# Graph layer with one-hot matmuls: all matmuls of a block in 128x32 tiles, and the normalisation in steps of its own

## The chip, the cores and the metric

The kernel runs on one core of a Trainium2 chip. The metric is the time of one execution on the device in microseconds; the kernel before takes 783.06 us (median of 3 runs, 783.03 to 785.78).

## What is computed

There are 6,250 nodes with 128 features and 100,000 edges, sorted by destination, of two types. Each edge sends its source's row, multiplied by one of two weight matrices, to its destination:

```python
Xs = X[src]
m_data = Xs @ W_data.T + b_data
m_ctrl = Xs @ W_control.T + b_control
msg = jnp.where((edge_types == 0)[:, None], m_data, m_ctrl)
agg = jax.ops.segment_sum(msg, dst, num_segments=X.shape[0])
out = jax.nn.relu(agg + (X @ W_self.T + b_self))
x = _layernorm(x + out, axis=-1)
```

## The kernel before

**Precision.** Every f32 value that goes through a matmul is kept as three bf16 parts whose sum is the value: `w3` (weights), `x3` (the transposed input), `m3` (the messages). A product of x and W is nine matmuls, one for each pair of parts.

**Prologue** (to about 118 us). The tables of messages are built for all nodes and both types: `multiply()` makes y = x W + b for a block of 128 nodes (L411, L414), `split_a` to `split_d` cut it into three parts in `m3`, which stays in SBUF: 98 tiles of 128 messages by 384 (three parts of 128). It also goes to a DRAM table. Constants are built at the start on VectorE while a transfer of the edges' rows (`er`) is under way.

**Groups.** Destinations are taken in 49 blocks of 128 nodes, in ten groups of 4, 5, 5, ... blocks. Before a group's blocks are summed its edges are put into slots: an edge of block q whose source lies in tile s of the 98 gets one of R = 32 slots of (q, s). A window of 18 x 128 edges per block is loaded. For each k of KT = 18, `bucket_hots` (L514, VectorE) makes `hot_st`, a one-hot of the source tile for 128 edges and all the blocks of the group, with the block index q innermost: reading one block's columns is a stride of n elements. `ranks` (L528 and L533, through the helper `by_columns` at L202, and L531) counts the slots. `fill_a` makes `two`, the one-hot of the slot times the source row and times the destination row. `fill_b` (L567) multiplies the two: for each k and q, `hot_st` is the stationary operand (128 columns), `two` is streamed (64 columns: 32 slots by two values). The result in PSUM holds, for every source tile, its slots' values.

`fill_c` copies it to `vs` (L580), writes the source rows to DRAM as `packed` (L582) in the order tile, slot, and turns the destination rows with small matmuls (L590) into `to`. Edges that found no slot are listed (to L661) and their messages fetched from the DRAM table into `msg_s` (32 rows), with `hot_s` as their one-hot of destinations.

**A block.** `spread` reads the block's row of `packed` back, broadcast to 128 partitions (`rows`, L697). `select` (L706, VectorE, two halves) turns it into one-hots of the source row. `to_hots` (L718) makes the one-hots of destinations, `hot_d`. Then for each of 25 buckets g of four source tiles: `gather` (L734) fetches the messages of 4 x 32 slots, each matmul with 32 columns of weights in its own column tile of TensorE; `evict` (L743, ScalarE) copies them as bf16 to `gs`; `add_up` (L753, through L202) adds them to the destinations in `agg` with `by_columns`, which cuts the 128 columns of weights into four matmuls of 32. The last bucket has 64 rows only. After it, one matmul of 32 rows by 128 columns adds the spilled edges (L757). `own_of` adds x W_self and its bias to the first 128 columns of `agg` (L774, L778). `finish_blocks` (VectorE) adds the three parts (L139), applies the relu and adds x (L135); after the last block of a group `norm_and_store` does the statistics, the root (ScalarE, L157), the scaling (L167) and the store (L172).

**Order.** [...] That order is made ahead of time by the planner `Order`: each `step` names the engines that can do it with their costs, what it needs, and (`due`) when it ought to be done. Steps emit their instructions when the planner picks them. The pools matter too: `agg` and `h_p` have one buffer, `g_ps` five, `gs` eight, `rows` four.

Of the kernel before, what the change touches and what calls it, by code (L numbers as in the profile page):

```python
# [38 lines left out]
NS = (NT + 3) // 4  # L39
PARTS = (4, 8, 8, 8, 8, 8, 5)  # L40
KC = 3
DC = 5
SC = 49
# [54 lines left out]
def kernel(  # L98
# [48 lines left out]
    def norm_and_store(h, b0, n, work):  # L147
        mv = work.tile([P, Q, 2], F32, name="mv")
        for j in range(n):
            st = work.tile([P, 6], F32, name="st")  # L150
            nc.vector.bn_stats(st, h[:, j, :])  # L151
            nc.vector.bn_aggr(mv[:, j, :], st)

        v = work.tile([P, Q], F32, name="v")
        nc.vector.tensor_scalar_add(v[:, :n], mv[:, :n, 1], EPS)
        s0 = work.tile([P, Q], F32, name="s0")
        nc.scalar.activation(s0[:, :n], v[:, :n], AF.Sqrt)  # L157
        r0 = work.tile([P, Q], F32, name="r0")
        nc.vector.reciprocal(r0[:, :n], s0[:, :n])
        q = work.tile([P, Q], F32, name="q")  # L160
        nc.vector.tensor_mul(q[:, :n], v[:, :n], r0[:, :n])
        nc.vector.tensor_add(q[:, :n], q[:, :n], s0[:, :n])
        rstd = work.tile([P, Q], F32, name="rstd")
        nc.vector.reciprocal(rstd[:, :n], q[:, :n])
        nc.vector.tensor_scalar_mul(rstd[:, :n], rstd[:, :n], 2.0)
        for j in range(n):
            nc.vector.tensor_scalar(h[:, j, :], h[:, j, :], mv[:, j, 0:1], rstd[:, j : j + 1],  # L167
                                    op0=ALU.subtract, op1=ALU.mult)
        n0 = b0 * P
        full = min(n, (N - n0) // P)  # L170
        if full:
            nc.sync.dma_start(  # L172
                out[n0 : n0 + full * P, :].rearrange("(b p) f -> p b f", p=P), h[:, :full, :]
            )
        if full < n:
            n1 = n0 + full * P
            nc.sync.dma_start(out[n1:N, :], h[: N - n1, full, :])

    with ExitStack() as main:
        sums_over_windows(main, tc, x, xt, edges, w, bias, table, x3_t, packed, total,  # L180
                          finish_parts, load_rows, norm_and_store)

    matched = nc.values_load(total[0:1, 0:1])
    with tc.If(matched != E), ExitStack() as rest:
        sums_over_all(rest, tc, xt, edges, w, bias, table, dram, finish, load_rows, norm_and_store)


def sums_over_windows(ctx, tc, x, xt, edges, w, bias, table, x3_t, packed, total,
                      finish_parts, load_rows, norm_and_store):
# [5 lines left out]
    ctx.enter_context(tc.manual_schedule())  # L195
    order = Order()
# [73 lines left out]
    V.tensor_scalar(rest, tri_f, -1.0, 1.0, op0=ALU.mult, op1=ALU.add)  # L270

    sel = const.tile([P, 4, NS], BF16, name="sel")
    for t in range(4):
        V.tensor_scalar(sel[:, t, :], iota_f[:, t + 1 : t + 1 + 4 * NS : 4], pid, None, op0=ALU.is_equal)
# [15 lines left out]
    three_parts([parts[:, i, :] for i in range(3)], b3, left[:3])  # L290
    bias3 = const.tile([3, D3], BF16, name="bias3")
# [50 lines left out]
    def due(kind, *i):  # L342
        if kind in ("counted", "turned", "first"):
            return 5.0
# [15 lines left out]
        if kind in ("rows", "sel", "d", "g", "e", "s"):  # L360
            of = {"rows": 1, "sel": 2, "d": 5}.get(kind, NS)
            lead = {"rows": -9, "sel": -3, "d": -1, "g": 0, "e": 1, "s": 2}[kind]
            return BUILT + BLOCK * (i[0] + (i[1] / of if len(i) > 1 else 0)) + lead
        n = GROUPS[i[0]]
        end = BUILT + BLOCK * STARTS[i[0]] - AHEAD
        if kind == "norm":
            return end + AHEAD + BLOCK * n + 20
# [187 lines left out]
    def fill_b():  # L555
        for grp, n in enumerate(GROUPS):
            free = [("listed", grp - 1)] if grp else ["first"]
            for c in range(KT // KC):
                yield step(("v", grp, c), {"T": 0.2 + 0.047 * KC * n}, ("two", grp, c), *free)
                if c == 0:  # L560
                    vts[grp] = ps_a.tile([P, 512], F32, name="small")
                vt = vts[grp][:, : n * 2 * R].rearrange("p (q r) -> p q r", q=n)
                two = two_s.pop((grp, c))
                for k in range(c * KC, c * KC + KC):
                    hot = hots.pop((grp, k))
                    for q in range(n):
                        T.matmul(vt[:, q, :], hot[:, :, q],  # L567
                                 two[:, k - c * KC, :, :, q].rearrange("p i r -> p (i r)"),
                                 start=k == 0 and q == 0, stop=k == KT - 1, skip_group_check=True)
                free = []  # L570

    def fill_c():
        for grp, n in enumerate(GROUPS):
# [3 lines left out]
            yield step(("vs", grp), {"A": 0.45}, ("v", grp, KT // KC - 1))  # L577
            vs = work.tile([P, Q, 2 * R], BF16, name="vs")
            vt = vts.pop(grp)
            A.copy(vs[:, :n, :], vt[:, : n * 2 * R].rearrange("p (q r) -> p q r", q=n))  # L580
            yield step(("packed", grp), {"S": 0.2}, ("vs", grp), lag=2.5)
            nc.sync.dma_start(  # L582
                packed[b0 : b0 + n, :].rearrange("q (s r) -> s q r", r=R), vs[1 : NT + 1, :n, :R]
            )
            yield step(("vd", grp), {"T": 0.05 * 4 * n}, ("vs", grp))
            vd = ps_a.tile([P, 512], F32, name="small")
            vd_v = vd[:, : n * NS].rearrange("p (q g) -> p q g", q=n)
            for q in range(n):
                for t in range(4):
                    T.matmul(vd_v[t * R : (t + 1) * R, q, :], vs[:, q, R:], sel[:, t, :],  # L590
                             start=True, stop=True, skip_group_check=True)
# [53 lines left out]
            for c in range(m):  # L645
# [14 lines left out]
            hot_s = work.tile([R, Q * P], BF16, name="hot_s")  # L660
            V.tensor_scalar(hot_s[:, : n * P], iota_f[:R, : n * P], dq, None, op0=ALU.is_equal)  # L661
            yield step(("spilled", grp), {"G": 0.8}, ("listed", grp), *stored, lag=2.5)
            msg_s = work.tile([R, D3], BF16, name="msg_s")
            G.indirect_dma_start(  # L664
                out=msg_s, out_offset=None, in_=table[:, :],
                in_offset=bass.IndirectOffsetOnAxis(ap=row_i[:, 0:1], axis=0),
            )
            spills[grp] = hot_s, msg_s
# [18 lines left out]
    d_hots, g_tiles, gs_tiles, aggs, xss, x3b, hs_ = {}, {}, {}, {}, {}, {}, {}  # L687
# [3 lines left out]
    def spread():  # L691

        for b, (grp, q) in enumerate(blocks):
            free = [("g", b - RB, NS - 1)] if b >= RB else []
            yield step(("rows", b), {"S": 0.1}, ("packed", grp), "built", *free, lag=4.0)
            rows[b] = late.tile([P, NT, R], BF16, name="rows", bufs=RB)
            nc.sync.dma_start(rows[b].rearrange("p s r -> p (s r)"),  # L697
                              packed[b : b + 1, :].to_broadcast([P, NT * R]))

    def select():  # L700

        for b in range(NB):
            for s0 in range(0, NT, SC):
                yield step(("sel", b, s0 // SC), {"V": 0.62}, ("rows", b))
                s = rows[b][:, s0 : min(s0 + SC, NT), :]
                V.tensor_scalar(s, s, pid1, None, op0=ALU.is_equal)  # L706
# [20 lines left out]
    def gather():  # L727
        for i, (b, g) in enumerate(tiles):
            free = [("e", *tiles[i - GB])] if i >= GB else ["built"]
            n = slots_of(g)  # L730
            yield step(("g", b, g), {"T": 0.17}, ("sel", b, (4 * g + n // R - 1) // SC), *free)
            g_tiles[b, g] = g_ps = ps_g.tile([P, 512], F32, name="g_ps")
            for t in range(n // R):
                T.matmul(g_ps[t * R : (t + 1) * R, :D3], rows[b][:, 4 * g + t, :],  # L734
# [10 lines left out]
    def add_up():  # L745
        for b, g in tiles:
            grp, q = blocks[b]
            free = [("agg", b)] if g == 0 else [("spilled", grp), ("o", b)] if g == NS - 1 else []
            yield step(("s", b, g), {"T": 0.17}, ("e", b, g), ("d", b, g // DC), *free)
# [5 lines left out]
            if g == NS - 1:  # L755
                hot_s, msg_s = spills[grp]
                T.matmul(aggs[b], hot_s[:, q * P : (q + 1) * P], msg_s, start=False, stop=True,  # L757
                         skip_group_check=True)
# [9 lines left out]
    def own_of(blocks, begun):  # L768

        for i, b in enumerate(blocks):  # L770
            yield step(("agg", b), {"S": 0.0}, *([("sum", blocks[i - 1])] if i else []))
            yield step(("o", b), {"T": 0.8}, ("xs", b), begun(b))
            own = aggs[b][:, :D]
            T.matmul(own, ones_b[:3, :], bias3[:, 2 * D :], start=False, stop=False,  # L774
                     skip_group_check=True)
            for i in range(3):
                for k in range(3):
                    T.matmul(own, x3b[b][:, i, :], w3[:, k, 2 * D :], start=False, stop=False,  # L778
                             skip_group_check=True)

    def finish_blocks():
        for b, (grp, q) in enumerate(blocks):
            yield step(("sum", b), {"V": 0.85}, ("s", b, NS - 1))
            if q == 0:
                hs_[grp] = late.tile([P, Q, D], F32, name="h_p")
            finish_parts(hs_[grp][:, q, :], aggs.pop(b), xss.pop(b), work)
            if q == GROUPS[grp] - 1:
                yield step(("norm", grp), {"V": 0.5 * GROUPS[grp] + 0.9}, ("sum", b))
                norm_and_store(hs_.pop(grp), STARTS[grp], GROUPS[grp], work)
# [4 lines left out]
    def close_build():  # L794
# [8 lines left out]
        spread(), select(), finish_blocks(), add_up(), gather(), evict(), to_hots(), bucket_hots(),  # L803
# [12 lines left out]
def sums_over_all(ctx, tc, xt, edges, w, bias, table, dram, finish, load_rows, norm_and_store):  # L816
# [3 lines left out]
    ps = ctx.enter_context(tc.tile_pool(name="ps_all", bufs=1, space=PSUM))  # L820
    w_self = const.tile([D, D], F32, name="w_self")
# [63 lines left out]
    for b0 in range(0, NB, Q):  # L885
        n = min(Q, NB - b0)
        h = work.tile([P, Q, D], F32, name="h")
        for j in range(n):
# [9 lines left out]
        norm_and_store(h, b0, n, work)  # L898
# [31 lines left out]
```

## Time and profile before

| | busy us | share of the span |
|---|---|---|
| TensorE matmuls | 718.1 | 92% |
| VectorE | 658.4 | 84% |
| ScalarE | 543.1 | 69% |
| GpSimd | 55.1 | 7% |

The costliest groups of instructions, with busy time, mean of one, and the idle time ahead of them with what ended it:

```profile
L743 ACT CAST gs<-g_ps 128x384 bf16<-128x384 f32 x1225 | 492.3, 498 | 136.2 <-PE g_ps L734 117.7
L734 PE MATMUL g_ps<-m,rows 128*32 128x384 bf16 x4802 | 381.8, 328 | 3.7 <-DVE rows L706 3.3
L718 DVE TENSOR_TENSOR hot_d<-count,to 128x640 bf16<-128x640 bf16 x245 | 132.6, 552 | 16.0 <-PE agg L202 12.3
L706 DVE TENSOR_SCALAR rows<-rows,pid 128x1568 bf16<-128x1568 bf16 x98 | 60.7, 621 | 0.7 <-DMA rows<-packed 0.7
L567 PE MATMUL small<-two,hot_st 128*128 128x64 bf16 x882 | 76.3, 255 | 4.4 <-DVE two L552 4.4
L778 PE MATMUL agg<-w,x_p 128*128 128x128 bf16 x441 | 33.1, 220 | 0.0
```

In a shape such as 128*32 128x384 the first pair is rows by columns of the weights, the second the streamed operand. Matmuls overlap, so the busy time of a group is the time in which at least one runs, and count times mean is much more. PE means TensorE, PEld its weight loads, DVE VectorE, ACT ScalarE, POOL GpSimd, SP the queue from which most transfers start.

### The profile page before, as it was taken

How to read it: one execution, taken by the hardware profiler on the slowest of the kernel's cores; microseconds unless marked ns; L12 is line 12 of the kernel's file. 1: busy time of each engine (PE TensorE's matmuls, PEld its weight loads, DVE VectorE, ACT ScalarE, POOL GpSimd, SP SyncE). 2: the span in 40 equal slices, each digit the busy share in tenths (PEclk: the TensorE clock that was granted, in tenths of full speed). 3: DMA queues.
4: the chain of work that ended last, by engine and by line, in shares of the span. 5: the costliest groups of instructions: out<-in, count | busy, mean ns of one | idle time of the engine just before them, and what ended most of it. 6: DMA issues, size and time to landing. Idle time of an engine off the chain costs nothing.

```text
span 783.7 us, 31989 instructions
## 1 busy us (share of the span) xinstructions
PE 718.1 (92%) x13451; PEld 474.0 (60%) x13451; DVE 658.4 (84%) x1764; ACT 543.1 (69%) x1321; POOL 55.1 (7%) x48
## 2 busy tenths in 40 slices
PE   0989949999999999999999999999998998999993
PEld 0556635665666666566656666666665665666662
DVE  6688878998989998998989899899998999968622
ACT  1445425687787679678777858767786786787993
POOL 2454420000000000000000000000000000000000
PEclk9999978999999999999999999999999999999997
DMA  5455463133105213310431520142052023205200
GB/s 198 121 169 184 165 215 124 25 122 105 44 15 178 74 27 137 112 24 16 176 75 27 181 71 21 32 161 78 16 181 74 11 69 124 82 12 181 69 3 20
DMA packets 60616, 72.93 MB, mean 93 GB/s; under 512 B 15348, under 2 KB 53249, under 8 KB 60417
## 3 DMA queue, kind: packets, MB, share of 16 engines
q1 hardware_dynamic: 58860, 66.69, 25.9%
q10 hardware_dynamic: 1158, 3.41, 1.2%
q8 instruction: 107, 1.75, 0.9%
q0 software_dynamic: 448, 0.72, 0.3%
q14 instruction: 43, 0.35, 0.1%
HBM read 52.85 MB, written 17.96 MB: 90 GB/s over the span
## 4 chain that ended last, share of the span: by engine, by line
PE 70%; DVE 21%; DMA 4%; issue 2%; ACT 1%; SPq 0%; POOL 0%; DVEq 0%; ACTq 0%
PE agg L202 22%; PE g_ps L734 20%; PE small L567 9%; PE acc L202 7%; PE y L414 6%; DVE slot L531 4%; DVE hot_d L718 3%; PE agg L778 3%; DVE rows L706 2%; DVE two L552 2%; PE agg L757 1%; DMA out<-h_p 1%; DMA er<-in_edges,row_i 1%; DMA rows<-packed 1%; DVE st L151 1%
## 5 line engine op out<-in xcount | busy, mean ns | idle before, releaser
L743 ACT CAST gs<-g_ps 128x384 bf16<-128x384 f32 x1225 | 492.3, 498 | 136.2 <-PE g_ps L734 117.7
L202 PE MATMUL agg<-gs,hot_d 128*32 128x384 bf16 (+1 forms) x4900 | 390.1, 332 | 15.7 <-ACT gs L743 15.3
L734 PE MATMUL g_ps<-m,rows 128*32 128x384 bf16 x4802 | 381.8, 328 | 3.7 <-DVE rows L706 3.3
L202 PEld LDWEIGHTS <-hot_d 128*32 128x32 bf16 (+1 forms) x4900 | 179.0, 114 | 103.5 <-issue 33.5
L734 PEld LDWEIGHTS <-rows 128*32 128x32 bf16 x4802 | 143.8, 98 | 61.8 <-issue 12.1
L718 DVE TENSOR_TENSOR hot_d<-count,to 128x640 bf16<-128x640 bf16 x245 | 132.6, 552 | 16.0 <-PE agg L202 12.3
L531 DVE TENSOR_REDUCE slot<-acc 128x5 f32<-128x490 f32 (+1 forms) x180 | 117.6, 653 | 28.3 <-PE acc L202 28.2
L514 DVE TENSOR_TENSOR hot_st<-count,st_b 128x640 bf16<-128x640 bf16 (+1 forms) x180 | 99.3, 568 | 3.1 <-PE small L567 3.1
L567 PE MATMUL small<-two,hot_st 128*128 128x64 bf16 x882 | 76.3, 255 | 4.4 <-DVE two L552 4.4
L567 PEld LDWEIGHTS <-hot_st 128*128 128x128 bf16 x882 | 65.8, 122 | 21.3 <-issue 20.1
L202 PE MATMUL acc<-hot_st,rest 128*32 128x490 bf16 (+1 forms) x720 | 69.9, 371 | 6.7 <-DVE slot L531 6.7
L202 PE MATMUL acc<-hot_st,tri 128*32 128x490 bf16 (+1 forms) x720 | 69.5, 368 | 0.0
L414 PE MATMUL y<-w,x 128*128 128x256 bf16 x441 | 62.9, 292 | 0.4 <-POOL x L397 0.4
L706 DVE TENSOR_SCALAR rows<-rows,pid 128x1568 bf16<-128x1568 bf16 x98 | 60.7, 621 | 0.7 <-DMA rows<-packed 0.7
L139 DVE TENSOR_REDUCE whole<-agg 128x128 f32<-128x384 f32 x49 | 27.2, 556 | 31.4 <-PE agg L757 30.4
L664 POOL DMA_INDIRECT msg_s<-table,row_i x10 | 9.9, 990 | 599.1 <-PE g_ps L734 533.3
L414 PEld LDWEIGHTS <-x 128*128 128x128 bf16 x441 | 41.3, 103 | 13.8 <-issue 1.3
L202 PEld LDWEIGHTS <-rest 128*32 128x32 bf16 x720 | 25.3, 95 | 26.1 <-issue 16.1
L439 ACT CAST m<-yr 128x512 bf16<-128x512 f32 (+1 forms) x25 | 15.2, 609 | 26.5 <-DVE yr L433 26.2
L778 PE MATMUL agg<-w,x_p 128*128 128x128 bf16 x441 | 33.1, 220 | 0.0
L552 DVE TENSOR_TENSOR two<-hr,lo 128x480 bf16<-128x480 bf16 (+1 forms) x60 | 29.0, 484 | 2.1
L552 DVE TENSOR_TENSOR two<-hr,rel_b 128x480 bf16<-128x480 bf16 (+1 forms) x60 | 30.6, 511 | 0.0
(135 smaller groups left out, 449.0 us busy)
## 6 DMA issues: line engine op xcount, KB each, us to landing
rows<-packed SPq DMA_DIRECT2D x49, 784.0 KB
table<-m SPq DMA_DIRECT2D x10, 768.0 KB
x_p<-x_t SPq DMA_DIRECT2D x49, 96.0 KB
x_t<-x SPq DMA_DIRECT2D x5, 768.0 KB
xs_p<-in_x SPq DMA_DIRECT2D x49, 64.0 KB
xt<-in_xt ACTq DMA_DIRECT2D x5, 512.0 KB
out<-h_p SPq DMA_DIRECT2D x8, 320.0 KB
win<-in_edges SPq DMA_DIRECT2D x49, 27.0 KB
```

The costliest lines, as they stand in the source:

```text
L139: nc.vector.tensor_reduce(whole, agg.rearrange("p (i c) -> p c i", i=3), axis=AX.X, op=ALU.add)
L202: T.matmul(out[c : c + 32], lhsT[:, c : c + 32], rhs, **flags)
L414: T.matmul(y[:, j, :], x3s[g][:, b + j - at_part[g], i, :], w3[:, k, : 2 * D], start=False, stop=i == k == 2)
L514: V.tensor_tensor(hot, counted[n], fields[grp][2][:, k, None, :].to_broadcast([P, P, n]), op=ALU.is_equal)
L531: V.tensor_reduce(slots[grp][:, k, :], by_q, axis=AX.X, op=ALU.max)
L552: V.tensor_tensor(two[:, :, i], hr, f[:, ks, None, :].to_broadcast(wide), op=ALU.mult)
L567: T.matmul(vt[:, q, :], hot[:, :, q], two[:, k - c * KC, :, :, q].rearrange("p i r -> p (i r)"), start=k == 0 and q == 0, stop=k == KT - 1 ...
L706: V.tensor_scalar(s, s, pid1, None, op0=ALU.is_equal)
L718: V.tensor_tensor(hot, counted[DC], places[grp][:, q, None, c * DC : c * DC + DC].to_broadcast([P, P, DC]), op=ALU.is_equal)
L734: T.matmul(g_ps[t * R : (t + 1) * R, :D3], rows[b][:, 4 * g + t, :], m3[:, 4 * g + t, :], start=True, stop=True)
L743: (A.copy if e == "A" else V.tensor_copy)(gs[:n], g_tiles.pop((b, g))[:n, :D3])
L778: T.matmul(own, x3b[b][:, i, :], w3[:, k, 2 * D :], start=False, stop=False, skip_group_check=True)
```

## The change

Within a block and its slots, matmuls with 128 columns of weights alternate with those of 32. The change gives those of the slots, of x W_self and of the spilled edges the shape of 128 rows by 32 columns:

- Slots: the operands are swapped. `two` (32 slots of one value of one block) is stationary, `hot_st` is streamed (100 source tiles). Two blocks share a PSUM range, in four column tiles. The result is turned round: slots on partitions, source tiles along the row. So `vs`, `packed` and `rows` are in the order slot, tile, and the weights of `gather` are read from `rows` with a stride of 98 elements. `select` is one instruction a block.
- x W_self: the three parts of the weights are streamed together (384 columns), into all three thirds of `agg`, which are added up later anyway.
- Spilled edges: `hot_s` and `msg_s` are padded to 128 rows; the rows past the 32 are zero but for one that holds the bias of W_self, which replaces L774.
- Normalisation: the statistics are taken after each block. Root, scale, apply and store are planner steps of their own, and the scaling of the rows goes from VectorE to ScalarE as an activation with scale and shift.

```diff
-                yield step(("v", grp, c), {"T": 0.2 + 0.047 * KC * n}, ("two", grp, c), *free)
+                yield step(("v", grp, c), {"T": 0.05 * KC * n}, ("two", grp, c), *free)
...
-                    hot = hots.pop((grp, k))
+                    hot = hots.pop((grp, k))[:, 1 : NC + 1, :]
                     for q in range(n):
-                        T.matmul(vt[:, q, :], hot[:, :, q],
-                                 two[:, k - c * KC, :, :, q].rearrange("p i r -> p (i r)"),
-                                 start=k == 0 and q == 0, stop=k == KT - 1, skip_group_check=True)
+                        for i in range(2):
+                            c0 = (q % 2 * 2 + i) * R
+                            T.matmul(vt[c0 : c0 + R, q // 2, :], two[:, k - c * KC, i, :, q],
+                                     hot[:, :, q], start=k == 0 and q < 2, stop=k == KT - 1,
+                                     skip_group_check=True)
...
-            A.copy(vs[:, :n, :], vt[:, : n * 2 * R].rearrange("p (q r) -> p q r", q=n))
+            A.copy(vs[:, : n // 2, :], vt[:, : n // 2, :])
+            if n % 2:
+                A.copy(vs[: 2 * R, n // 2, :], vt[: 2 * R, n // 2, :])
...
-            for s0 in range(0, NT, SC):
-                yield step(("sel", b, s0 // SC), {"V": 0.62}, ("rows", b))
-                s = rows[b][:, s0 : min(s0 + SC, NT), :]
-                V.tensor_scalar(s, s, pid1, None, op0=ALU.is_equal)
+            yield step(("sel", b), {"V": 1.2}, ("rows", b))
+            V.tensor_scalar(rows[b], rows[b], pid1, None, op0=ALU.is_equal)
...
-                T.matmul(g_ps[t * R : (t + 1) * R, :D3], rows[b][:, 4 * g + t, :],
+                T.matmul(g_ps[t * R : (t + 1) * R, :D3], rows[b][:, :, 4 * g + t],
                          m3[:, 4 * g + t, :], start=True, stop=True)
...
-                T.matmul(aggs[b], hot_s[:, q * P : (q + 1) * P], msg_s, start=False, stop=True,
-                         skip_group_check=True)
+                by_columns(aggs[b], hot_s[:, q * P : (q + 1) * P], msg_s, start=False, stop=True,
+                           skip_group_check=True)
...
-            own = aggs[b][:, :D]
-            T.matmul(own, ones_b[:3, :], bias3[:, 2 * D :], start=False, stop=False,
-                     skip_group_check=True)
             for i in range(3):
-                for k in range(3):
-                    T.matmul(own, x3b[b][:, i, :], w3[:, k, 2 * D :], start=False, stop=False,
-                             skip_group_check=True)
+                by_columns(aggs[b].rearrange("p (i c) -> p i c", i=3), x3b[b][:, i, :],
+                           w3[:, :, 2 * D :], start=False, stop=False, skip_group_check=True)
...
-            nc.vector.tensor_scalar(h[:, j, :], h[:, j, :], mv[:, j, 0:1], rstd[:, j : j + 1],
-                                    op0=ALU.subtract, op1=ALU.mult)
+            nc.scalar.activation(h[:, j, :], h[:, j, :], AF.Identity,
+                                 bias=shift[:, j : j + 1], scale=rstd[:, j : j + 1])
...
+        for grp, (get, b0, n) in enumerate(group):
+            yield step((last, "root", grp), {"V": 0.2}, ("sum", b0 + n - 1))
+            h, mv = get()
+            v, s0 = root(mv, n, work)
+            yield step((last, "rooted", grp), {"A": 0.3}, (last, "root", grp))
+            yield step((last, "scale", grp), {"V": 1.0}, (last, "rooted", grp))
+            scales = scale(mv, v, s0, n, work)
+            yield step((last, "apply", grp), {"A": 0.28 * n}, (last, "scale", grp))
+            apply(h, *scales, n)
+            yield step((last, "out", grp), {"S": 0.3}, (last, "apply", grp))
+            store_out(h, b0, n)
```

## The prediction

> **What bounds the kernel now.** I read the busy shares first, then the busy time by stage, then the chain that ended last, then one stretch of the steady state instruction by instruction.
>
> ```profile
> PE 718.1 (92%) x13451; PEld 474.0 (60%) x13451; DVE 658.4 (84%) x1764; ACT 543.1 (69%) x1321; POOL 55.1 (7%) x48
> ```
>
> Two engines are heavily loaded, so a share over the whole span does not decide. By stage (columns: length, then busy us and count of PE, PEld, DVE, ACT, POOL, then clock, DMA share, GB/s):
>
> ```profile
> 200.00:300.00 100.00, 97.60 (x1977) 64.78 (x1973) 91.05 (x241) 77.40 (x195) 0.91 (x1) 1.00 0.19 61
> 740.00:784.00 44.00, 31.29 (x622) 19.99 (x622) 12.15 (x39) 28.78 (x76) 0.00 (x0) 0.89 0.04 11
> ```
>
> In the steady state TensorE is the bound, with VectorE only 6.5 points behind. In the tail VectorE is nearly idle, and ScalarE stands close to TensorE. The chain agrees:
>
> ```profile
> PE 70%; DVE 21%; DMA 4%; issue 2%; ACT 1%; SPq 0%; POOL 0%; DVEq 0%; ACTq 0%
> ```
>
> The ScalarE square roots of the normalisation come once per group: 325.1, 392.5, 460.8, 527.9, 595.3, 663.5 us. So a group of five blocks takes (663.5 - 325.1)/5 = 67.7 us. From the first window that is 66.0 us of TensorE, 61.6 of VectorE, 52.4 of ScalarE a group: 1.7 us are lost.
>
> The stretch (start us, us, engine, line, operation, names, rows*columns of the weights, columns streamed, count):
>
> ```profile
> 405.34 0.35 PE L202 MATMUL agg<-gs,hot_d 128*32 128x384 bf16 x4
> 405.51 0.35 PE L734 MATMUL g_ps<-m,rows 128*32 128x384 bf16 x4
> 405.79 1.31 PE L567 MATMUL small<-two,hot_st 128*128 128x64 bf16 x15
> 407.03 0.37 PE L202 MATMUL agg<-gs,hot_d 128*32 128x384 bf16 x4
> ...
> 421.91 0.49 PE L734 MATMUL g_ps<-m,rows 128*32 128x384 bf16 x4
> 422.33 0.36 PE L202 MATMUL agg<-gs,hot_d 64*32 64x384 bf16 x4
> 422.62 0.33 PE L757 MATMUL agg<-msg_s,hot_s 32*128 32x384 bf16 x1
> 422.89 0.39 PE L202 MATMUL acc<-hot_st,rest 128*32 128x490 bf16 x4
> ...
> 424.29 0.82 PE L202 MATMUL agg<-gs,hot_d 128*32 128x384 bf16 x16
> 425.04 0.22 PE L774 MATMUL agg<-bias,ones_b 3*128 3x128 bf16 x1
> 425.20 0.68 PE L778 MATMUL agg<-w,x_p 128*128 128x128 bf16 x9
> 425.81 0.37 PE L202 MATMUL agg<-gs,hot_d 128*32 128x384 bf16 x4
> ```
>
> Starts count here, not durations: four 384-column matmuls in four column tiles start 0.162 us after the four before them (405.34 to 405.51), so the four run side by side at 0.42 ns a column. At every change of shape there is a hole of about 0.1 us.
>
> **What the Trainium skill says.** (1) "TensorEngine Tiling (Array Packing)", Key Properties: changing the tiling mode, not just the tile, drains TensorE. The trace agrees: the 64-row group starts 0.42 us after the group before it, not 0.16. (2) "SBUF — State Buffer", the note on cachelines: SBUF is read in 16-byte lines, and each crossing to a new line pays. The slot step (L567) reads both operands strided. With four blocks in the group (8 bytes apart) twelve take 0.91 us, so (0.91 - 0.255)/11 = 60 ns each; with five (10 bytes) (1.31 - 0.255)/14 = 75 ns. The contiguous L778, with twice the columns, has (0.68 - 0.22)/8 = 57 ns. So strided reads do cost, in proportion to the stride; the trace does not say which operand pays. (3) "ScalarE: Activation LUTs", What ACT_TABLE_LOAD costs: an activation with two pointer operands on 128 columns is 280 + 107 + 93 ns, less 93 back to back, an estimate of 0.39 us. The nearest rows agree: casts of 125 and 384 columns take 267 and 498 ns. Its section on table sets says identity is in every set, so I charge no table load.
>
> **The change part by part, per group of five blocks.**
>
> W_self x: rounds of four 128x32 matmuls replace ten 128x128 matmuls. Before: the sixteen agg matmuls end their slot at 424.29 + 4 x 0.162 = 424.94, the next slot starts at 425.81: 0.87 us. After: 12 matmuls of 384 columns, three rounds, 3 x 0.162 = 0.49, no change of shape. Five blocks: -1.9 us of TensorE.
>
> Spilled edges: before, 422.07 to 422.89 is 0.82 us for the 64-row group and the spill. The 64-row group stays, with its own holes; after: 0.26 + 0.29 + 0.16 = 0.71. Five blocks: -0.55.
>
> Slots: before, from 405.67 to 407.03 is 1.36 us for a step of three k. After: 30 matmuls of 100 columns instead of 15 of 64, in four column tiles. Blocks 0, 2, 4 share tiles 0 and 1, so a step has 3 x 3 = 9 rounds. If the weights paid for the stride, a round is 100 x 0.42 = 42 ns and the step 0.4 us; if the streamed operand did, it is 75/64 x 100 = 117 ns and the step 1.05. I take 1.05, since a 10-byte stride stays on the streamed side, and the 128-column loads show only 25 ns more than contiguous ones (hot_st 122, x_p 98 ns). Six steps: -1.9, with -5.8 as the good end. The bad end is column tiles that cannot stream strided data together: two at a time is 15 x 117 = 1.76, +2.4.
>
> Gather weights: rows is now read with a stride of 196 bytes, one line for each of 32 weights. In the groups
>
> ```profile
> L202 PEld LDWEIGHTS <-hot_d 128*32 128x32 bf16 x4704 | 172.5, 115 | 87.1 <-issue 17.1
> L734 PEld LDWEIGHTS <-rows 128*32 128x32 bf16 x4802 | 143.8, 98 | 61.8 <-issue 12.1 <-DVE rows L706 0.2
> ```
>
> a 10-byte stride (20 lines, not 4) adds 17 ns, and the agg rounds still come every 162 ns. 32 lines then add 28/16 x 17 = 30 ns to a load that takes 22 ns a tile (twenty L590 loads in 0.20 us): 52 ns, hidden by the 162 ns stream if the four tiles load side by side. Cost 0.
>
> TensorE: 66.0 - 1.9 - 0.55 - 1.9 = 61.6.
>
> VectorE: the five final scalings leave (1.37 us for five at 393.8); ten selects become five of double length, saving between 0 and the 0.17 us that the smallest operations take: -0.1 each, -0.5; one shift operation is added, +0.2. Stats only move. 61.6 - 1.37 - 0.5 + 0.2 = 59.9.
>
> ScalarE: five applies, 5 x 0.39 = +1.95, and a second slot copy, +0.25: about 54.6, not a bound. Behind the applies in its queue stand evictions, for which TensorE waits; but the 1.95 us for which ScalarE now waits at the square root (the value row v is delayed by VectorE's block of statistics) goes, and the order puts five or six evictions between root and apply. I charge nothing net. The single h_p buffer must be stored before the next group's first write: apply 2 us and store 3.9 us, and 22 VectorE instructions (about 10 us) stand in between, where eight did, with a wait of 0.95. Free. The second write of packed costs 0.4 us on the queue ahead of rows; one more hot_d of 0.47 us stands ahead of the select that waits for it. Free.
>
> Period: two engines at 61.6 and 59.9 lose a little more than 1.7 us between them, say 2.1: 63.7, so -4.0 a group.
>
> Sum: seven full groups, -28. The first group (72 us, four blocks) and the last but one (61.5): -3 each. The last group has no slot work, and ScalarE's 25 evictions of 0.395 us make 9.9 us of each 10.3 us block: -0.4 x 5 = -2. Prologue: slot steps with a four-block group save six times 0.3, and about 2.3 us of new VectorE set-up fits in its 3.0 us wait for the er transfer: -1. End: statistics of four blocks (0.39 each) are done earlier, the applies are slower by 0.6, the shift is 0.2: -0.8. Together -38: **745 us**.
>
> **The rivals.** A, the above, 0.60. B: the streamed stride is free. TensorE falls to 57.7, VectorE at 59.9 is the bound, period 61.5: -6.2 x 7, -5 -5 -2 -2.5 -0.8 = -59, 724 us. For it: 32-column tiles may read apart; against: the 60 and 75 ns. 0.15. C: strided streams in different tiles hinder each other. Between A and the bad end, TensorE falls by 0 to 4.4 and the time is 745 to 780. For it: only contiguous streams are seen side by side. 0.14. D: slower. The strided gather loads are taken one tile after another, 4 x 52 = 208 ns, and the gather round goes from 162 to 208: +46 x 125 = +5.8 us a group, period 69.5, +1.8 x 8, and +1.1 - 0.4 for each of the last blocks, less prologue and end: about 800 us. Against: twenty loads in 0.20 us run side by side. 0.09. The rest is for an order of queues that loses what is saved.
>
> The range holds A, B nearly whole and most of C: 723 to 775. Faster by over 0.5% are A, B and nine tenths of C: 0.87; same 0.03; slower 0.10.
>
> **What would show it.** TensorE busy in the steady state falling to 96% or less with VectorE at 93 to 95; agg with 384 streamed columns from w in rounds of 0.162 us; a slot step of 1.05 us (0.4 is B, 1.5 or more C); gather rounds still at 0.162 us (D if over 0.18); ScalarE applies near 0.39 us; root to root 63.7 us. It is wrong if a new wait, of VectorE on h_p or of TensorE on the evictions behind the applies, exceeds 1 us a group.

## The result and the profile after

The changed kernel takes 757.65 us (median of 4 runs, 757.46 to 758.82) against 783.04 for the kernel before: a ratio of 0.9673, with a 95% interval of 0.9647 to 0.9699. That is faster by 25 us; 745 was forecast, in a range of 723 to 775. The two profiled runs span 755.7 and 783.7 us, 28 us apart, since the profiled run of before lies at the upper end of its spread (785.43 us).

The same views as for before, first the page's busy shares, then the busy time in the steady state, then the chain that ended last:

```profile
PE 694.5 (92%) x14578; PEld 553.7 (73%) x14578; DVE 645.1 (85%) x1683; ACT 563.0 (74%) x1379; POOL 58.5 (8%) x48
```

```profile
200.00:300.00 100.00, 98.20 (x2265) 81.95 (x2257) 91.19 (x254) 83.37 (x212) 1.64 (x1) 1.00 0.23 72
```

```profile
PE 66%; DVE 28%; DMA 2%; issue 2%; ACT 1%; POOL 0%; ACTq 0%; DVEq 0%
```

The shares look almost as before, and that is the trap in them: TensorE does less, yet is "98% busy" in a shorter period. A matmul of 384 columns is shown with 0.33 to 0.35 us, while the next four on the same column tiles start after 0.16, so a matmul's modelled end lies about 0.17 us after its last column, and shorter holes do not show as idle. The chain tells more: VectorE's part has grown from 21 to 28%.

Where the time came from, by a landmark that both kernels have, ScalarE's copy of a group's slot values out of PSUM:

| stretch | before, us | after, us | gain |
|---|---|---|---|
| start to the first copy | 109.25 | 105.86 | 3.4 |
| first to third copy | 125.45 | 122.61 | 2.8 |
| third to tenth copy, seven groups | 473.03 | 453.83 | 19.2 |
| one of these groups | 67.58 | 64.83 | 2.75 |
| tenth copy to the last reduction L139 | 63.50 | 62.02 | 1.5 |
| from there to the end | 12.5 | 11.4 | 1.1 |

The stretch of matmuls that answers to the one of before (start, us, engine, line, operation, names, shape, count):

```profile
403.07 0.35 PE L768 MATMUL g_ps<-m,rows 128*32 128x384 bf16 x4
403.24 0.99 PE L600 MATMUL small<-hot_st,two 128*32 128x100 bf16 x26
403.94 0.36 PE L216 MATMUL agg<-gs,hot_d 128*32 128x384 bf16 x2
404.03 0.32 PE L600 MATMUL small<-hot_st,two 128*32 128x100 bf16 x2
404.14 0.33 PE L768 MATMUL g_ps<-m,rows 128*32 128x384 bf16 x2
404.15 0.33 PE L600 MATMUL small<-hot_st,two 128*32 128x100 bf16 x2
404.27 0.38 PE L216 MATMUL agg<-gs,hot_d 128*32 128x384 bf16 x2
...
408.32 0.36 PE L768 MATMUL g_ps<-m,rows 128*32 128x384 bf16 x2
408.61 0.36 PE L216 MATMUL agg<-gs,hot_d 64*32 64x384 bf16 x4
408.90 0.35 PE L216 MATMUL agg<-msg_s,hot_s 128*32 128x384 bf16 x4
409.08 0.38 PE L216 MATMUL acc<-hot_st,rest 128*32 128x490 bf16 x4
...
411.45 0.71 PE L216 MATMUL agg<-w,x_p 128*32 128x384 bf16 x12
411.94 0.39 PE L216 MATMUL agg<-gs,hot_d 128*32 128x384 bf16 x4
```

The slot step begins at 403.24; the next matmuls come at 404.27 on two of the column tiles: 1.03 us. They come at 403.94 on the other two, which have six matmuls in the step and not nine. x W_self takes 411.45 to 411.94, 0.49 us with no hole around it.

The operations that were new or changed (line, engine, operation, names, shapes, count, then busy us and mean ns, then the idle time ahead):

```profile
L768 PEld LDWEIGHTS <-rows 128*32 128x32 bf16 x4802 | 241.3, 136 | 41.8 <-issue 15.3 <-DVE rows L740 6.5
L740 DVE TENSOR_SCALAR rows<-rows,pid 128x3136 bf16<-128x3136 bf16 x49 | 50.4, 1028 | 0.2
L176 ACT ACTIVATE h_p<-h_p,shift,rstd 128x128 f32<-128x128 f32 x49 | 20.1, 503 | 1.3 <-DVE shift L170 1.3
```

The strided weight loads are longer (136 ns against 98), as expected, the double select takes 1.03 us, and five applies take 2.04 us (at 311.00), 0.41 each.

Now the waits. From 228 to 680 us, a stretch of nearly seven groups in both kernels, who waited for whom (engine and line, releaser, us in total, times, longest), in the kernel before:

```profile
PE agg L202 <- ACT gs L743: 11.4, 11, 1.5
PE acc L202 <- DVE slot L531: 2.5, 8, 0.5
DVE whole L139 <- PE agg L757: 7.4, 18, 0.9
```

and in the changed one:

```profile
PE acc L216 <- DVE slot L561: 5.4, 14, 0.6
PE g_ps L768 <- DVE rows L740: 3.7, 7, 0.7
DVE whole L139 <- PE agg L216: 15.1, 19, 1.0
```

The wait of the agg matmuls for evictions is gone from the list: it stood behind ScalarE's wait at the square root, and comes back with the old normalisation (below). In its place TensorE waits for VectorE's slot reductions and selects, and VectorE twice as long for finished sums. The two hinder each other in turn.

This list leaves out waits shorter than a matmul's modelled tail. Counting starts brings them in. This is an estimate: each matmul is charged 0.42 ns for each column that it streams through its column tile (1.17 in a slot step that streams with a stride), and each hole over 40 ns in a column tile (counted as a quarter of TensorE) goes to the engine whose signal came last, where that was within 0.15 us of the start. In the seven groups, the holes that VectorE ended come to 1.4 us of TensorE's time a group before and 3.2 after, those that ScalarE ended to 2.5 and 1.8. So VectorE's part has more than doubled. ScalarE's has not vanished: 1.2 of its 1.8 us are gathers that start when an eviction has freed a buffer of `g_ps`.

### The profile page after: what moved, and what is told of

It is laid out like the page before. It is cut to its first block, busy times and chain, and to the rows that moved or that the text cites. A ratio compares the mean times of both kernels' runs of the same rounds, so it can differ in the third digit from the quotient of the medians.

```text
span 755.7 us, 34248 instructions
## 1 busy us (share of the span) xinstructions
PE 694.5 (92%) x14578; PEld 553.7 (73%) x14578; DVE 645.1 (85%) x1683; ACT 563.0 (74%) x1379; POOL 58.5 (8%) x48
## 4 chain that ended last, share of the span: by engine, by line
PE 66%; DVE 28%; DMA 2%; issue 2%; ACT 1%; POOL 0%; ACTq 0%; DVEq 0%
PE agg L216 24%; PE g_ps L768 20%; PE acc L216 9%; PE small L600 6%; PE y L444 6%; DVE slot L561 4%; DVE hot_d L752 4%; DVE hot_st L544 2%; DVE two L582 2%; DVE whole L139 2%; DMA rows<-packed 1%; DVE hr L577 1%; DVE rows L740 1%; PE y L441 1%; DVE st L149 1%
## 5 line engine op out<-in xcount | busy, mean ns | idle before, releaser
L768 PE MATMUL g_ps<-m,rows 128*32 128x384 bf16 x4802 | 412.1, 331 | 5.9 <-DVE rows L740 5.9
L216 PE MATMUL agg<-gs,hot_d 128*32 128x384 bf16 (+1 forms) x4900 | 412.7, 331 | 1.8 <-ACT gs L777 1.6
L768 PEld LDWEIGHTS <-rows 128*32 128x32 bf16 x4802 | 241.3, 136 | 41.8 <-issue 15.3
L216 PEld LDWEIGHTS <-hot_d 128*32 128x32 bf16 (+1 forms) x4900 | 225.8, 115 | 37.9 <-issue 21.0
L561 DVE TENSOR_REDUCE slot<-acc 128x5 f32<-128x490 f32 (+1 forms) x180 | 116.8, 649 | 17.3 <-PE acc L216 11.4
L216 PE MATMUL acc<-hot_st,tri 128*32 128x490 bf16 (+1 forms) x720 | 89.8, 371 | 2.7 <-DVE full L708 2.7
L600 PE MATMUL small<-hot_st,two 128*32 128x100 bf16 x1764 | 76.1, 294 | 3.4 <-DVE two L582 2.6
L600 PEld LDWEIGHTS <-two 128*32 128x32 bf16 x1764 | 62.9, 119 | 10.6 <-DVE two L582 9.2
L139 DVE TENSOR_REDUCE whole<-agg 128x128 f32<-128x384 f32 x49 | 27.2, 555 | 38.3 <-PE agg L216 29.7
L740 DVE TENSOR_SCALAR rows<-rows,pid 128x3136 bf16<-128x3136 bf16 x49 | 50.4, 1028 | 0.2
L216 PE MATMUL agg<-w,x_p 128*32 128x384 bf16 x588 | 37.2, 326 | 0.0
L216 PEld LDWEIGHTS <-tri 128*32 128x32 bf16 x720 | 30.3, 97 | 6.0 <-issue 4.0
```

The lines of the kernel that those rows point to most:

```text
L139: nc.vector.tensor_reduce(whole, agg.rearrange("p (i c) -> p c i", i=3), axis=AX.X, op=ALU.add)
L216: T.matmul(out[c : c + 32], lhsT[:, c : c + 32], rhs, **flags)
L561: V.tensor_reduce(slots[grp][:, k, :], by_q, axis=AX.X, op=ALU.max)
L600: T.matmul(vt[c0 : c0 + R, q // 2, :], two[:, k - c * KC, i, :, q], hot[:, :, q], start=k == 0 and q < 2, stop=k == KT - 1, skip_group_che ...
L740: V.tensor_scalar(rows[b], rows[b], pid1, None, op0=ALU.is_equal)
L768: T.matmul(g_ps[t * R : (t + 1) * R, :D3], rows[b][:, :, 4 * g + t], m3[:, 4 * g + t, :], start=True, stop=True)
```

## The experiments

They were run in three rounds on three chips, each round with its own runs of the kernel before on the same chip (780.98, 783.12 and 782.85 us), so I compare ratios; the change itself is 0.9673. The group period is the mean of the seven groups between the third and the tenth copy, in the one profiled run of each kernel. The two kernels with plain weights, which time like the change, have periods within 0.11 us of its period.

| kernel | time, us | ratio, 95% interval | period, us |
|---|---|---|---|
| the change | 757.65 | 0.9673 (0.9647 to 0.9699) | 64.83 |
| plain stream in the slot step | 739.19 | 0.9458 (0.9427 to 0.9489) | 62.92 |
| plain weights in the slot step | 756.34 | 0.9677 (0.9643 to 0.9711) | 64.72 |
| plain weights in gather | 756.05 | 0.9673 (0.9639 to 0.9707) | 64.81 |
| no x W_self | 751.78 | 0.9618 (0.9587 to 0.9649) | 64.45 |
| no statistics | 746.42 | 0.9525 (0.9492 to 0.9557) | 63.74 |
| neither | 735.96 | 0.9405 (0.9390 to 0.9421) | 62.68 |
| normalisation of before | 767.45 | 0.9798 (0.9764 to 0.9832) | 66.33 |
| x W_self of before | 761.71 | 0.9717 (0.9681 to 0.9752) | 65.43 |
| slots of before | 772.53 | 0.9851 (0.9807 to 0.9896) | 66.19 |
| AHEAD = 16 | 762.00 | 0.9744 (0.9719 to 0.9769) | 65.04 |
| checks on GpSimd | 757.46 | 0.9680 (0.9641 to 0.9718) | 64.90 |
| both of the last two | 761.69 | 0.9743 (0.9723 to 0.9763) | 65.14 |

### Which operand of the slot step pays for its stride

```diff
-                                     hot[:, :, q], start=k == 0 and q < 2, stop=k == KT - 1,
+                                     hot.rearrange("p s q -> p (s q)")[:, q * NC : (q + 1) * NC],
+                                     start=k == 0 and q < 2, stop=k == KT - 1,
```

> The changed kernel, but the slot step streams 100 neighbouring elements of hot_st instead of every fifth one (the slots' values are then not those of the edges; the same number and shape of instructions, in the same order). Theory 1 (the streamed operand pays for the stride, about 1.17 ns a column against 0.42): the slot step falls from about 1.05 us on column tiles 0 and 1 to about 0.42 us, TensorE is relieved of 3.8 us a group; VectorE (59.6 us a group) then binds, a period of 62 us against 64.9, time 733 to 738 us. Theory 2 (the stationary operand pays): the step and the time stay as they are, 756 to 759.

The streamed operand pays. In the timeline of the plain stream the step begins at 403.78 and the next matmul on the slow column tiles, those with nine, at 404.19:

```profile
403.78 0.54 PE L600 MATMUL small<-hot_st,two 128*32 128x100 bf16 x27
404.11 0.38 PE L769 MATMUL g_ps<-m,rows 128*32 128x384 bf16 x2
404.14 0.22 PE L600 MATMUL small<-hot_st,two 128*32 128x100 bf16 x2
404.19 0.33 PE L769 MATMUL g_ps<-m,rows 128*32 128x384 bf16 x1
```

That is 0.41 us for nine rounds, 46 ns a round, against 1.03 us or 114 ns with the 10-byte stride. The step was as expected under theory 1. The time gained is 17 us by the ratio, a little less than expected, and a group gains 1.9 us where TensorE lost 3.7 us of work. VectorE is then 93.8% busy (281.35 of the 300 us from 200 on), and by the count of starts VectorE ends 4.9 us of TensorE's holes a group where it was 3.2.

```diff
-                            T.matmul(vt[c0 : c0 + R, q // 2, :], two[:, k - c * KC, i, :, q],
+                            T.matmul(vt[c0 : c0 + R, q // 2, :],
+                                     two[:, k - c * KC, i].rearrange("p r q -> p (r q)")[:, q * R : (q + 1) * R],
```

> The changed kernel, but the slot step loads 32 neighbouring elements of two as weights instead of every fifth one (values wrong for the edges, same instructions). Theory 1: load times fall from 119 to about 97 ns, the step stays at 1.05 us, time 756 to 759. Theory 2: the step falls to about 0.5 us, time about 735.

No change (0.9677 against 0.9673): the weights' stride costs nothing here that the time shows, though their loads fall from 119 to 110 ns.

### Whether the strided weights of gather cost anything

```diff
-                T.matmul(g_ps[t * R : (t + 1) * R, :D3], rows[b][:, :, 4 * g + t],
+                T.matmul(g_ps[t * R : (t + 1) * R, :D3],
+                         rows[b].rearrange("p r s -> p (r s)")[:, (4 * g + t) * R : (4 * g + t + 1) * R],
```

> The changed kernel, but the weights of gather are 32 neighbouring elements of rows instead of elements 196 bytes apart (a permutation of the slots, values wrong; same instructions). Theory 1 (the loads hide behind the 0.162 us rounds): the loads fall from 136 to about 98 ns, the time stays within 2 us of 757.6. Rival (strided loads cost something after each wait, where they can not be taken ahead): two or three exposures of 40 ns a block would give 752 to 754, and slow rounds throughout 740.

The loads fall to 98 ns and neither ratio nor period moves. Whatever the longer loads take is hidden behind the rounds.

### Which engine binds

```diff
             for i in range(3):
-                by_columns(aggs[b].rearrange("p (i c) -> p i c", i=3), x3b[b][:, i, :],
-                           w3[:, :, 2 * D :], start=False, stop=False, skip_group_check=True)
```

> The changed kernel without the matmuls of x W_self (left out: that product; its bias stays). TensorE has 0.49 us a block less, 24 us in all. If TensorE alone binds the steady state: 735. If VectorE alone binds it: 756 to 758 but for the tail, so 754. If the two hinder each other in turn (theory 1: 61.6 and 59.6 us a group, period 64.9): about half, 743 to 748.

Of 2.45 us of TensorE in a group, 0.4 show: less than a shared bound was expected to give. The waits from 228 to 680 us say where the rest went:

```profile
PE acc L216 <- DVE slot L561: 11.9, 32, 0.6
```

TensorE arrives earlier at the next rank matmul and waits there for VectorE: 11.9 us where it was 5.4, and 32 times where it was 14. With the short waits, by the count of starts, the holes that VectorE ended grow from 3.2 to 4.9 us a group: 1.7 of the 2.1 us that do not show.

```diff
+                V.memset(mvs[grp], 1.0)
...
-            stats(mvs[grp][:, q, :], hs_[grp][:, q, :], work)
```

> The changed kernel without the statistics of each block (left out: mean and variance, a constant stands for them). VectorE has 0.30 + 0.18 us a block less, 2.4 us a group. Theory V (new: after the change the path runs through VectorE most of the time, TensorE's 97% busy is slack in part): nearly all of it shows, period 62.5 to 63, time 737 to 742. Theory T (TensorE still binds): 753 to 756, only the tail gains.

Both theories were too simple. Of 2.4 us of VectorE, 1.1 show. TensorE's busy share rises to 98.6% (295.93 of 300 us) and its wait for slot reductions falls below what the list shows. By the count of starts the holes that VectorE ended fall from 3.2 to 2.3 us a group. So VectorE was in front, but TensorE stood close behind it.

> The changed kernel without the matmuls of x W_self and without the statistics of each block (both left out, as in the two runs that left out one each). Theory C (new: two nearly equal bounds; taking from one exposes the other): without statistics TensorE was 98.6% busy, so here its 2.45 us a group should count nearly in full on top of that run's 746.4: 724 to 731, more than the two single gains together (-11 and -5 from 757.6, that is 742). Theory V (VectorE alone): 743 to 746, the tail's 2 us.

Without statistics, taking x W_self away saves 1.06 us a group; with them it saved 0.38. The two gains together are 2.15 us a group where the single ones add up to 1.47; in the ratio 0.0268 where they add up to 0.0203, a difference little above what the intervals allow. This is what theory C says in kind, though not in size: 735.96 is between its 724 to 731 and the 743 to 746 of VectorE alone. ScalarE, at 53 us of the 62.68, was lightened in no run, so how much of what is left is its part is open.

### The parts of the change undone, one at a time

The first takes back the step `normalise` for `norm_and_store`, with its due time:

```diff
...
-            stats(mvs[grp][:, q, :], hs_[grp][:, q, :], work)
...
+            if q == GROUPS[grp] - 1:
+                yield step(("norm", grp), {"V": 0.5 * GROUPS[grp] + 0.9}, ("sum", b))
+                norm_and_store(hs_.pop(grp), STARTS[grp], GROUPS[grp], work)
...
```

> The changed kernel with the normalisation of before (one VectorE step after a group's last block, rows scaled on VectorE). VectorE has 1.2 us a group more, in one block of about 5 us, and ScalarE waits for it. Theory V: 1.2 us a group and more, 767 to 772. Theory T: 757 to 760.

Theory V's figure: +1.5 us a group, 9.8 us in all. From 228 to 690 us ScalarE waits for VectorE ahead of the square root, and TensorE for evictions again:

```profile
ACT s L200 <- DVE v L198: 13.7, 7, 2.0
PE agg L240 <- ACT gs L803: 10.3, 7, 1.5
DVE h_p L135 <- DMA out<-h_p: 5.5, 3, 2.4
```

The first is two us in each group, during which no eviction runs; in the changed kernel it is 1.7 us in all, and the second is not on its list. The third is a wait of VectorE until `h_p` is stored. In the kernel before it is 0.9 us, so this run takes back a little more than the change did.

```diff
...
-                by_columns(aggs[b].rearrange("p (i c) -> p i c", i=3), x3b[b][:, i, :],
-                           w3[:, :, 2 * D :], start=False, stop=False, skip_group_check=True)
+                for k in range(3):
+                    T.matmul(own, x3b[b][:, i, :], w3[:, k, 2 * D :], start=False, stop=False,
+                             skip_group_check=True)
```

> The changed kernel with x W_self as nine 128x128 matmuls a block, as before (the bias stays in the padded spill). TensorE has about 0.35 us a block more, 1.8 us a group. Theory V, from the run without these matmuls (2.45 us a group less gave 0.3): mostly absorbed, 757 to 763. Theory T (the prediction's -1.9 a group counts in full): 772.

+0.6 us a group of 1.8 us of work: mostly absorbed. The profiled run is the slowest of the four (764.41 us), so 0.6 may be too much. By the ratios it is 3.4 us in all, and the intervals of this kernel and of the change overlap.

```diff
...
-                            T.matmul(vt[c0 : c0 + R, q // 2, :], two[:, k - c * KC, i, :, q],
-                                     hot[:, :, q], start=k == 0 and q < 2, stop=k == KT - 1,
...
+                        T.matmul(vt[:, q, :], hot[:, :, q],
+                                 two[:, k - c * KC, :, :, q].rearrange("p i r -> p (i r)"),
...
```

> The changed kernel with the slots of before: hot_st stationary, 128x128 matmuls, rows in the order tile, slot, two selects a block. TensorE has 6 x 0.31 = 1.9 us a group more and VectorE 0.3 to 0.5. From the plain stream (3.8 us a group less gave 1.75) theory V expects +0.9 and +0.4 a group, 765 to 770. Theory T: +1.9 a group, 774. Rival (swapping gave nothing, since the streamed operand pays for its stride): 756 to 759.

+1.36 us a group and 15 us in all, the largest of the three and more than theory V expected in all; the group's 1.36 is what it expected. The first copy comes 4.1 us later (109.92 against 105.86), so some of the rest is in the prologue. Shape changes, drains and the doubled selects come back together here, and this run does not part them.

The three sum to 3.5 us a group, where the whole change is worth 2.75. Two bounds would make them overlap so, but the wait for `h_p`, 0.8 us a group that only the first of these runs has, is as large as the difference.

### Attempts at a faster version

```diff
-    AHEAD = 12.0
+    AHEAD = 16.0
```

> The changed kernel with AHEAD = 16 instead of 12: the planner wants a group's slots 4 us earlier, so that packed, rows and the select are not the last thing that the next group's first gather waits for (TensorE waits 5.9 us in all for rows, ten times). Theory H (the hand-over between groups costs 0.5 to 1 us each): 749 to 754. Theory C (two full engines, the order hardly matters): 756 to 759.

Theory H fails: the period is 0.2 us longer, and the whole 4 us. The hand-over is not free, though. TensorE's wait for the selects falls from 3.7 to 1.0 us (228 to 680 us), and a new one takes its place, which the changed kernel's list does not have:

```profile
PE small L657 <- DVE flags L652: 8.9, 7, 1.4
```

Most of the loss comes early: counted by the last reduction of a group, 3.4 of the 4.7 us between the profiled runs are lost by the end of the second group.

```diff
...
-            V.tensor_reduce(most, n_over, axis=AX.X, op=ALU.max)
-            V.tensor_single_scalar(bad[:, 1:2], most, 2.5, op=ALU.is_ge)
...
+            G.tensor_single_scalar(bads[:, grp, :n], n_over, 2.5, op=ALU.is_ge)
...
```

> The changed kernel with eight small VectorE instructions a group (the checks for overfull slots, about 1.5 us a group) replaced by three on GpSimd, whose flags are added up once at the end. Same result. By the run without statistics (2.4 us of VectorE a group gave 1.1) theory V and theory C expect 0.6 to 0.7 us a group, 750 to 753. Theory T (only TensorE counts): 757. If GpSimd disturbs VectorE: 758 or more.

Nothing, against theories V and C. The instructions that leave VectorE are seven, not eight, and took 1.1 us a group. VectorE's other operations take as long as in the changed kernel (`hot_d` 552 ns against 553, `hot_st` 550 against 552), so GpSimd did not slow them. The freed time became waits of VectorE for TensorE:

```profile
DVE slot L565 <- PE g_ps L770: 12.3, 28, 1.2
```

In the changed kernel the same wait is 3.2 us, 12 times. The planner moved steps in this run; which move made the waits is open.

> Both: the checks on GpSimd and AHEAD = 16. If the two gains are of different waits they add: 743 to 749. If not, as the better of the two.

As AHEAD alone. None of the versions that give the full result beats the change.

## Why the prediction was right, and where it was off

- **Direction and mechanism: right.** Each of the three parts taken back makes the kernel slower by itself, the slots and the normalisation clear of the noise, x W_self within it. Two forecast signs did not come: TensorE busy at 96% or less and VectorE at 93 to 95% became 97.6 and 91.6% (292.88 and 274.89 of the 300 us from 200 on), since waits too short to show as idle count as busy TensorE.
- **x W_self, 0.87 to 0.49 us: right as work** (411.45 to 411.94). In the time it is worth least, 3 to 4 us.
- **Slot step, 1.05 us: right**, 1.03, and right in its reason: the streamed operand pays, 114 ns a round where 117 was reckoned. Rival B needed the weights to pay; the two plain kernels refute that. Rival C is refuted by the same 114 ns: four strided streams side by side are no slower than one was.
- **Spilled edges, 0.82 to 0.71 us: both too dear, their difference nearly right.** The row at 421.91 holds two pairs of gathers, and the second pair starts at 422.07. So the 64-row group starts 0.26 us after it, not 0.42, and the hole is 0.1 us. Counted from the end of the last pair, the median of 37 blocks is 0.65 us before and 0.56 after: 0.45 us a group where 0.55 was reckoned.
- **Gather weights at no cost: right**, shown by the plain gather. Rival D falls with it.
- **VectorE, 1.7 us a group less: right.** Over the seven whole groups its busy time falls from 60.7 to 58.9 us a group, 1.8 less; the prediction's 61.6 and 59.9 come from one window. The applies at 0.39 were 0.41.
- **ScalarE at no net cost: right in sign**, and its half of the argument was worth more than I charged: the listed wait of 11.4 us of TensorE for evictions disappeared, and the old normalisation costs 10 us. By the count of starts ScalarE's holes fell by 0.7 us a group, the new short waits of gathers included.
- **The term that was mis-sized is the loss between the two engines.** I let it grow by 0.4 us, from 1.7 to 2.1. TensorE's work fell by about 4.2 us a group, nearly the 4.35 of the sum (1.9 for x W_self, 0.45 for the spilled edges, 1.9 for the slots), and the period by 2.75, so the loss grew by about 1.4. That is 1.0 of the 1.25 us by which a gain of 4.0 a group became 2.75; the rest is the spilled edges and rounding. VectorE is where the growth sits: the holes in TensorE's starts that VectorE ended grew by 1.8 us a group. TensorE had been 4.6 us of busy time a group above VectorE (65.3 and 60.7); less those 4.2 it is about 2.2 above VectorE's 58.9. As the two draw level and each waits for the other's last result, more of the saved time turns into waits. The runs with one or both lightened show it: 0.38 us alone, 1.06 once VectorE was lightened too.
- **First groups, last groups, end:** -1 for the prologue was too little (3.4); the rest (-3, -3, -2) was somewhat too much: 2.8 from first to third copy and 1.5 from the tenth copy to the last reduction. The end was -1.1, not -0.8. That these parts come to 8.8 us where 9.8 was forecast is luck: their errors cancel. The prologue's gain comes with the slots, since with the slots of before the first copy is as late as it was (109.92 us).

## What to carry to other kernels

Price a saving by where the engine goes next, not by the engine's busy share: the same microsecond of TensorE was worth half in the slot step (1.9 of 3.7 us) and a sixth in x W_self (0.38 of 2.45). Why these two differ was not tested. Where two engines are within a few per cent of each other, add up both demands, take the larger, and expect the loss between them to grow as they draw level; here, taking work off both at once paid more than the sum (2.15 against 1.47 us a group). When swapping operands for a shape, look at which one is then streamed with a stride.

## What the runs showed that was not expected

Column tiles keep their own time. All 30 matmuls of a slot step stand before the agg matmuls in TensorE's program order, and yet two agg matmuls start at 403.94 on the tiles that are done, before the last four slot matmuls (404.03 and 404.15). The lead of a third of a microsecond lasts through the rounds that follow; whether it costs anything was not tested.

A streamed bf16 operand with a 10-byte stride runs at 1.14 ns a column against 0.46 in the same matmuls without one, four tiles side by side; 32-column weight loads with strides of 10 and of 196 bytes cost no time that the two runs with plain weights show (0.9677 and 0.9673 against 0.9673).
